# A planned two-layer transformer block: PSUM dependencies kept by bank, up and gate in banks of their own, identity products at the start, the first norm by halves

## The chip, the core and the metric

The kernel runs on one core of a Trainium2 chip. The time is device time in microseconds (us). Of the kernel before there are three runs: 910.86, 911.13 and 912.05, median 911.13. The engines are TensorE (PE; its weight loads are shown apart as PEld), VectorE (DVE), ScalarE (ACT), GpSimd (POOL), and SyncE (SP), whose queue issues the DMA transfers.

## The reference, cut to what matters

The input is x of 2 x 1024 tokens with 256 channels. Two layers follow each other; in each, attention and a feed-forward network read the same normed x and are both added to x.

```python
xn = layernorm(x)                          # layer 0
# linear attention, 16 heads of 16 channels: q' = elu(q) + 1, k' = elu(k) + 1
kv, z = sum_s k' v, q' . sum_s k'
att   = (q' kv / (z + 1e-6)) @ o_w.T + o_b
# feed-forward, 1024 wide, weights ternary: scale * round(w / scale) clipped to -1..1
ffn   = (silu(xn @ wu.T) * (xn @ wg.T)) @ wd.T      # scale = mean(|w|)
x     = x + att + ffn
xn = layernorm(x)                          # layer 1
att   = softmax(rope(q) rope(k).T / 4) v @ out_w.T + out_b
ffn   = up and gate of a signed Walsh-Hadamard transform of xn, silu(gate) * up,
        a second transform, down
x     = x + att + ffn
```

## The kernel before

Tokens are cut into four chunks of 512 (`xc[0]` to `xc[3]`, tiles x0 to x3; two for each batch). A chunk holds four groups of 128 tokens on the partitions. `norm_T` norms a chunk (DVE statistics, a power on POOL, `shift` on DVE, `xn` on ACT) and transposes it on PE into `xnT`, by way of two PSUM tiles `pt` that DVE and ACT copy out.

**The planned stage.** Everything of layer 0 but the last two feed-forward pieces, the first heads of layer 1 and the first search for peaks of scores is not issued as it is called. It is recorded: `record(group, ...)` runs a generator, and each call on PE, DVE, ACT or POOL becomes an `Op` of a `Plan` (consecutive PE calls up to a `cut` are one `Op`). `Plan.add` notes for every operation which earlier ones it needs, element by element of each tile (`Root`: writer, readers, adders). `Plan.emit` is a list scheduler: it gives each operation a length by `cost`, a hand-over by `LAT`, a priority that is its longest path to the end plus the constant that its group has for its engine in `LEADS`, and it takes a place of a tile only when its ring (`Ring`) has one free. It then issues all operations in the order found. `with_place` has an operation claim a place of a later tile already. `fetch` issues a load on SP's queue at once and notes an expected time of arrival. The list sets the order alone. The semaphores between engines come from the framework, which sees the issued order and the tiles.

In this stage the main groups are: `norm 0`, `norm 1` (the two chunks of batch 0); `project0` (`pq`, from which `r` and `e` are made on ACT and summed to q on POOL; `pkv`, from which DVE makes `kc` and ACT copies `va0`; then `ke` on ACT and `kp` on DVE); `state0` (`pk`, `kv`); `attend0` (`pa`, on DVE `rz` and `att0`; transposes to `attT`; `py`); `ternary` for `wuT0`, `wgT0` and `wdT0` (absolute values and sum on ACT, then a `pt` product over the partitions, then comparisons on DVE); the feed-forward pieces 0 to 3 with `wide=True` and 4 and 5 with `by_pool=True`; heads of layer 1 (`pqkv`, rope); the search parts.

A feed-forward piece is 256 tokens (F). `ffn0` goes over its 1024 hidden channels in blocks of 128, or in double blocks where `wide`. x is used as a sum of two single-precision-rounded parts (`xs`), so a block's up and gate are four matmuls of 256 columns each:

```python
for i in range(step):
    for w, weight in enumerate((wu, wg)):
        mm(pug[:, i, w, :], ...four products...)
scalar.activation(act, pug[:, :, 0, :], AF.Tanh, scale=su_half)
vector.scalar_tensor_tensor(act, act, 1.0, pug[:, :, 0, :], ALU.add, ALU.mult)
vector.scalar_tensor_tensor(act, pug[:, :, 1, :], sgd, act, ALU.mult, ALU.mult)
```

A wide `pug` is a `pair` tile, two PSUM banks of 512 numbers for each partition. There are two such pairs, three tiles of one bank (`bank`: `pt`, `pq`, `pkv`, `pk`, `pa`, `py`) and one, `po`.

**The main loop.** After the planned stage an order written out by hand runs eight units of attention of layer 1 (score products `scm` for the peaks, `sce` for the exponentials, `po` for the sums over v) with the rest of the feed-forward work as filler between them.

Nearly every instruction is issued through one helper, so the profile gives line L314 for all of them; groups are told apart by their tiles.

Of the kernel before, what the change touches and what calls it, by code (L numbers as in the profile page):

```python
# [21 lines left out]
P = 128  # L22
# [20 lines left out]


ENGINES = (PE, DVE, ACT, POOL)
LAT = {PE: 0.25, DVE: 0.18, ACT: 0.22, POOL: 0.15}
AHEAD = 2
LEADS = {
    "norm 0": (884, 880, 840, 780),
    "norm 1": (805, 801, 799, 770),  # L50
    "project 0": (801, 823, 823, 847),
    "project 1": (741, 1160, 919, 1000),
    "state 0": (313, 274, 323, 305),
    "attend 0": (829, 830, 806, 861),
    "attend 1": (437, 353, 368, 369),
    "wuT0": (878, 850, 751, 881),
    "wgT0": (831, 797, 770, 789),
    "wdT0": (266, 269, 300, 322),
    "piece 0": (199, 348, 389, 1041),
    "piece 1": (756, 826, 796, 770),  # L60
    "piece 2": (369, 405, 420, 380),
    "piece 3": (234, 206, 155, 167),
    "norm1 0": (367, 384, 381, 390),
    "heads 0": (303, 270, 292, 294),
    "norm1 1": (840, 853, 784, 848),
    "heads 1": (322, 272, 267, 216),
    "search 0": (216, 180, 148, 109),
    "search 1": (47, -87, 51, 13),
    "search 2": (325, 231, 328, 330),
    "search 3": (17, -6, -6, 1),  # L70
    "norm 2": (260, 224, 40, 189),
    "norm 3": (369, 226, 181, 113),
    "project 2": (245, 311, 212, 132),
    "project 3": (207, 182, 164, 210),
    "state 1": (35, 115, 42, 32),
    "attend 2": (836, 870, 861, 837),
    "attend 3": (185, 202, 198, 211),
    "piece 4": (324, 202, 297, 177),
    "piece 5": (185, 198, 238, 203),
}  # L80
FREE = ("stats", "mv", "rstd", "shift", "rz", "part")
BURST = 0.65
# [15 lines left out]
class Root:  # L98


    def __init__(self, make, n, dtype, ring, before):
        self.make, self.dtype, self.ring, self.before = make, dtype, ring, before
        self.tile = None
        self.sums = False
        self.placed = False
        self.ready = 0.0
        self.writer = np.full(n, -1)
        self.readers, self.adders, self.users = [], [], []

# [47 lines left out]
class Plan:  # L157
    def __init__(self):
        self.ops = []
        self.open = None  # L160
        self.burst = False
        self.group("norm 0")
        self.holds, self.later = [], set()

    def cut(self):
# [14 lines left out]
    def add(self, engine, call, name, args, kw):  # L180
        if engine == PE and self.open is not None:
            op = self.open
        else:
            op = Op(len(self.ops), engine, self.leads[ENGINES.index(engine)])
            self.ops.append(op)
            self.open = op if engine == PE else None
            if self.burst:
                op.cost = BURST
        op.calls.append((call, args, kw))
        for r in self.holds:  # L190
            self.use(op, r)
        self.holds.clear()
        op.needs.update(self.later)
        self.later.clear()
        outs = [args[0]] + ([kw["accum_out"]] if "accum_out" in kw else [])
        ins = [v for v in (*args[1:], *kw.values()) if isinstance(v, View) and v is not kw.get("accum_out")]
        if not self.burst:
            op.cost += cost(engine, name, outs[0], ins)
        for v in ins:
            r, ids = v.root, np.unique(v.ids)  # L200
            op.needs.update(r.writer[ids])
            if not (r.sums and outs[0].root is r):
                op.needs.update(i for i, other in r.adders if np.intersect1d(ids, other).size)
                r.readers.append((op.i, ids))
            self.use(op, r)
        for v in outs:
            r, ids = v.root, np.unique(v.ids)
            op.needs.update(r.writer[ids])
            op.needs.update(i for i, other in r.readers if np.intersect1d(ids, other).size)
            if r.sums and any(u.root is r for u in ins):  # L210
                r.adders.append((op.i, ids))
            else:
                op.needs.update(i for i, other in r.adders if np.intersect1d(ids, other).size)
                r.writer[ids] = op.i
            self.use(op, r)
        op.needs -= {-1, op.i}

    def use(self, op, r):
        op.ready = max(op.ready, r.ready)
        if r.tile is None and r not in op.roots:  # L220
            op.roots.append(r)
        r.users.append(op.i)
# [48 lines left out]
class Pool:  # L271


    def __init__(self, state, pool, bufs):
        self.state, self.pool, self.bufs, self.rings = state, pool, bufs, {}

    def tile(self, shape, dtype, tag, name, bufs=None):
        n = bufs or self.bufs
        ring = self.rings.setdefault(tag, Ring(n, tag not in ("bank", "pair", "stage", *FREE)))
        root = ring.latest = Root(  # L280
            lambda: self.pool.tile(list(shape), dtype, tag=tag, name=name, bufs=n),
            int(np.prod(shape[1:])),
            dtype,
            ring,
            ring.latest,
        )
# [52 lines left out]
def cost(engine, name, out, ins):  # L339
# [5 lines left out]
        return ins[1].ids.size * (PASS if single else COL)  # L345
    if engine == DVE:
        n = max([n] + [v.ids.size for v in ins if name in ("tensor_reduce", "bn_stats")])
        return n / 960 + 0.07 + (0.5 if name in ("tensor_scalar", "scalar_tensor_tensor") and n >= 1024 else 0.0)
    if engine == ACT:
        return n / 1200 + (0.05 if name == "copy" else 0.01 + 0.09 * len(ins))  # L350
    return n / 472 + (0.19 if n > 16 else 0.8)
# [3 lines left out]
def tile_two_layers(ctx: ExitStack, tc: tile.TileContext, a: dict, out: bass.AP):  # L355
# [10 lines left out]
    def open_pool(stack, name, bufs, **kw):  # L366
        return Pool(state, stack.enter_context(tc.tile_pool(name=name, bufs=bufs, **kw)), bufs)

    const = open_pool(ctx, "const", 1)
    small = open_pool(ctx, "small", 4)  # L370
    ps = open_pool(ctx, "ps", 1, space=PSUM)
    ident = const.tile([P, P], F32, tag="ident", name="ident")
    make_identity(nc, real(ident))
    plan = state.plan = Plan()


    def pair(name):
# [16 lines left out]
    def fetch(t, view):  # L394

        sync.dma_start(out=t, in_=view)
        fetched[0] += t.ids.size * P * 4
        t.root.ready = 3.4 + fetched[0] / 330e3

    def load_w(pool, name, k, n, tag=None):  # L400

# [10 lines left out]
        xc[c].root.sums = True  # L412
        xnT.append(const.tile([P, 2, C], F32, tag=f"xnT{c}", name=f"xnT{c}"))

    def load_x(c):
        fetch(xc[c], x_d[:, c * CT : (c + 1) * CT, :])

    ident_r = const.tile([P, P], F32R, tag="ident_r", name="ident_r")
    vector.tensor_copy(ident_r, ident)
# [1 line left out]
    vector.tensor_scalar(ones_r, ident, 0.0, 1.0, ALU.mult, ALU.add)  # L421
    minus_half = const.tile([P, CT], F32, tag="minus_half", name="minus_half")
    vector.memset(minus_half, -0.5)

    def mm(out_, pairs):
        for i, (lhsT, rhs) in enumerate(pairs):
# [3 lines left out]


    SOON, FIRST, SECOND, LAST, PAIR = 1, 2, 3, 4, 5

    def norm_T(src, dst, pause=0.0):

# [84 lines left out]
    sb = open_pool(l0, "sa", 1)  # L520


    load_x(0)
    wq = load_w(w0, "wqT0", D, D)
    qb = load(w0, "qb0", a["qb0"], [P, 2])
    minus_qb = w0.tile([P, 2], F32, tag="minus_qb", name="minus_qb")
# [34 lines left out]
    def project0(c):  # L561
# [126 lines left out]
    def ffn0(cc, before_down, wide=False, by_pool=False):  # L688
# [20 lines left out]
        for e in range(0, NB, step):  # L709
            act = (sb if wide else const).tile([P, step, F], F32, tag="act", name="act", bufs=2 if wide else 3)  # L710
            gate = const.tile([P, step, F], F32, tag="gate", name="gate", bufs=1) if by_pool else None
            if wide:
                pug = pair("pug").rearrange("p b (w n) -> p b w n", w=2)
            else:
                pug = bank("pug").rearrange("p (b w n) -> p b w n", b=1, w=2)
            for i in range(step):
                cols = slice((e + i) * P, (e + i + 1) * P)
                for w, weight in enumerate((wu, wg)):
                    if state.plan:
                        plan.with_place(act)  # L720
                        plan.with_place(gate)
                    mm(pug[:, i, w, :], [(weight[:, k, cols], xs[:, s, k, :]) for k in range(2) for s in range(2)])
                    if (i, w) != (step - 1, 1):
                        yield 4 * F * PASS
            scalar.activation(act, pug[:, :, 0, :], AF.Tanh, scale=su_half)
            if by_pool:

                scalar.mul(gate, pug[:, :, 1, :], sgd)
            if acts:
                split()  # L730
            yield 4 * F * PASS, SOON
            vector.scalar_tensor_tensor(act, act, 1.0, pug[:, :, 0, :], ALU.add, ALU.mult)
            if by_pool:
                gpsimd.tensor_tensor(act, act, gate, ALU.mult)
            else:
                vector.scalar_tensor_tensor(act, pug[:, :, 1, :], sgd, act, ALU.mult, ALU.mult)
            acts.append(act)
            yield 0.0
        before_down()
# [485 lines left out]
            plan.cut()  # L1225


    record("norm 0", norm_T(xc[0], xnT[0]))
# [168 lines left out]
```

## Time and profile before

| what | value |
|---|---|
| time, median of 3 runs | 911.13 us (910.86 to 912.05) |
| the profiled execution: its time | 910.88 us |
| the profiled execution: its span | 909.1 us (some 1.8 us lie outside it) |
| mean granted TensorE clock | 0.996 |
| PE busy in 0 to 213.0 us | 192.4 us |
| first `scm` matmul (end of the planned stage) | 213.0 us |
| HBM read, written | 11.75 MB, 2.10 MB |

A window row reads: start and end, length, then for PE, PEld, DVE, ACT and POOL the busy us and the number of instructions, then the granted clock, the DMA share and GB/s. A timeline row reads: start, duration, engine, line, operation, output <- inputs and shapes, how many; in brackets the idle time of the engine just before and what ended it. A row of the chain of waits reads: start, length, engine, tile, how many. A row of the waits reads: who waited for whom, total us, how often, the longest. Two matmul records stand for one fp32 product.

### The profile page before, as it was taken

How to read it: one execution, taken by the hardware profiler on the slowest of the kernel's cores; microseconds unless marked ns; L12 is line 12 of the kernel's file. 1: busy time of each engine (PE TensorE's matmuls, PEld its weight loads, DVE VectorE, ACT ScalarE, POOL GpSimd, SP SyncE). 2: the span in 40 equal slices, each digit the busy share in tenths (PEclk: the TensorE clock that was granted, in tenths of full speed). 3: DMA queues.
4: the chain of work that ended last, by engine and by line, in shares of the span. 5: the costliest groups of instructions: out<-in, count | busy, mean ns of one | idle time of the engine just before them, and what ended most of it. 6: DMA issues, size and time to landing. Idle time of an engine off the chain costs nothing.

```text
span 909.1 us, 14565 instructions
## 1 busy us (share of the span) xinstructions
PE 863.3 (95%) x6036; PEld 515.5 (57%) x6036; DVE 581.9 (64%) x954; ACT 439.2 (48%) x641; POOL 212.1 (23%) x279
## 2 busy tenths in 40 slices
PE   5988899999989998999999999999999999999997
PEld 2687766676556543554555555555555555555543
DVE  3895558886876786657765656677565666656212
ACT  5733565434655542444544444455444444444563
POOL 2525578433643140005500000154000000000000
PEclk9999999999999999999999999999999999999999
DMA  9100000000000110000000000000000000000001
GB/s 316 64 1 1 1 1 1 1 1 1 1 25 25 47 47 1 1 1 1 1 1 1 1 1 25 1 1 1 24 1 1 1 2 1 1 1 2 1 6 41
DMA packets 11297, 14.77 MB, mean 16 GB/s; under 512 B 1248, under 2 KB 8928, under 8 KB 11232
## 3 DMA queue, kind: packets, MB, share of 16 engines
q1 hardware_dynamic: 11232, 13.85, 4.6%
q8 instruction: 47, 0.77, 0.4%
q14 instruction: 18, 0.15, 0.1%
HBM read 11.75 MB, written 2.10 MB: 15 GB/s over the span
## 4 chain that ended last, share of the span: by engine, by line
PE 72%; DVE 21%; issue 3%; ACT 3%; DMA 1%; POOL 0%; SPq 0%; ACTq 0%; DVEq 0%; POOLq 0%
PE pug L314 19%; DVE peak L314 17%; PE scm L314 16%; PE py L314 13%; PE sce L314 7%; PE pqkv L314 4%; PE pt L314 4%; PE pkv L314 3%; PE pw L314 2%; PE po L314 2%; PE pq L314 1%; PE sc L314 1%; ACT pr L314 1%; DVE act L314 1%; ACT act L314 1%
## 5 line engine op out<-in xcount | busy, mean ns | idle before, releaser
L314 ACT ACTIVATE pr<-sce 128x1024 f32<-128x1024 f32 x256 | 260.2, 1023 | 269.4 <-PE sce L314 269.1
L314 DVE TENSOR_REDUCE peak<-scm 128x2 f32<-128x1024 f32 x224 | 274.0, 1223 | 167.6 <-PE scm L314 166.7
L314 PE MATMUL po<-pr,va 128*17 128x512 f32 x1024 | 135.6, 598 | 0.0
L314 PE MATMUL sce<-qk_hi 32*128 32x512 f32 x512 | 123.0, 495 | 4.7 <-ACT pr L314 2.3
L314 PEld LDWEIGHTS scm<-qk_hi 32*128 32x128 f32 x448 | 41.4, 182 | 151.4 <-DVE peak L314 113.8
L314 PE MATMUL scm<-qk_hi 32*128 32x512 f32 x448 | 111.9, 496 | 12.0 <-DVE peak L314 1.0
L314 POOL CAST tops<-nm 128x16 fp32r<-128x16 f32 x16 | 3.4, 213 | 409.4 <-DVE nm L314 405.6
L314 PE MATMUL sce<-ql,qk_hi 32*128 32x512 f32 x512 | 97.0, 393 | 0.0
L314 PE MATMUL sce<-mx,ones_r 32*128 32x512 f32 x512 | 96.7, 391 | 0.1
L314 PE MATMUL scm<-qk_hi,ql 32*128 32x512 f32 x448 | 89.1, 394 | 0.0
L314 DVE SCALAR_TENSOR_TENSOR act<-act,pug 128x256 f32<-128x256 f32 (+1 forms) x112 | 50.8, 454 | 58.2 <-ACT act L314 32.6
L314 PE MATMUL pug<-xnT,eff_wgT 128*128 128x256 f32 x256 | 69.2, 392 | 0.0
L314 PE MATMUL pug<-xnT,eff_wuT 128*128 128x256 f32 x256 | 68.3, 382 | 0.0
L314 PE MATMUL py<-wd,hid 128*128 128x256 f32 x256 | 63.2, 388 | 0.0
L314 POOL TENSOR_TENSOR hid<-act,hid 128x256 fp32r<-128x256 f32 (+1 forms) x48 | 44.1, 921 | 68.9 <-ACT hid L314 40.7
L314 ACT ACTIVATE act<-pug,ws_ug 128x256 f32<-128x256 f32 x64 | 30.3, 474 | 55.3 <-PE pug L314 55.3
L314 PEld LDWEIGHTS pug<-xnT,eff_wgT 128*128 128x128 f32 x256 | 45.5, 189 | 16.5 <-issue 10.6
L314 PEld LDWEIGHTS py<-wd,hid 128*128 128x128 f32 x256 | 46.4, 190 | 14.8 <-issue 8.6
L314 PEld LDWEIGHTS sce<-qk_hi 32*128 32x128 f32 x512 | 45.9, 181 | 15.6 <-ACT pr L314 9.7
L314 PEld LDWEIGHTS pug<-xnT,eff_wuT 128*128 128x128 f32 x256 | 47.9, 190 | 9.8 <-issue 2.6
L314 PEld LDWEIGHTS sce<-mx,ones_r 32*128 32x128 f32 x512 | 46.6, 183 | 11.0 <-ACT mx L314 0.5
L314 PE MATMUL pqkv<-wqkvT,xnT 128*128 128x384 f32 x128 | 49.0, 505 | 2.2 <-DVE ql L314 1.6
(144 smaller groups left out, 1310.4 us busy)
## 6 DMA issues: line engine op xcount, KB each, us to landing
x<-in_x SPq DMA_DIRECT2D x4, 512.0 KB, 7.1
out<-x SPq DMA_DIRECT2D x16, 128.0 KB, 1.7
both<-in_wuT SPq DMA_DIRECT2D x1, 1024.0 KB, 8.6
both<-in_wgT SPq DMA_DIRECT2D x1, 1024.0 KB, 10.7
wdT<-in_wdT SPq DMA_DIRECT2D x1, 1024.0 KB, 13.0
raw<-in_wdT SPq DMA_DIRECT2D x2, 512.0 KB, 3.5
raw<-in_wgT SPq DMA_DIRECT2D x2, 512.0 KB, 3.4
raw<-in_wuT SPq DMA_DIRECT2D x2, 512.0 KB, 3.3
```

Of the source, the lines that this page charges most:

```text
L314: return call(*map(real, args), **{k: real(v) for k, v in kw.items()})
```

## The change

- `open_pool` and `Pool` hand a `grain` to each `Root`. For the PSUM pool it is 512 (C), a bank; the plan's dependencies of PSUM tiles are then noted by bank and no longer by element. Arrival times (`ready`) are noted for each element.
- In `ffn0` a wide block's `pug` is laid out with up first (all of bank 0) and gate second (all of bank 1), and the loops are exchanged: up of both halves, then gate of both.
- Fourteen fp32 products of `ident` with itself go to PE ahead of the plan, which is now created after them.
- `xc[0]` is loaded in two transfers and normed by `norm_halves`: two token groups at a time, from the statistics to the transposed copy (DVE copies the first half, ACT the second).
- `cost` has other lengths for long DVE operations, `LAT` has 0.1 in place of 0.15 for POOL, `project0` calls `with_place` for q, `kc` and `va0`, and all constants of `LEADS` are new.

```diff
-LAT = {PE: 0.25, DVE: 0.18, ACT: 0.22, POOL: 0.15}
+LAT = {PE: 0.25, DVE: 0.18, ACT: 0.22, POOL: 0.1}
 LEADS = {
-    "norm 0": (884, 880, 840, 780),
-    "norm 1": (805, 801, 799, 770),
-    "project 0": (801, 823, 823, 847),
+    "norm 0a": (1268, 1283, 1353, 1307),
+    "norm 0b": (1266, 1278, 1247, 1252),
+    "norm 1": (1210, 1162, 1187, 1148),
+    "project 0": (1056, 1212, 1220, 1354),
...
         for v in ins:
-            r, ids = v.root, np.unique(v.ids)
+            r, ids = v.root, np.unique(v.ids // v.root.grain)
...
-        return n / 960 + 0.07 + (0.5 if name in ("tensor_scalar", "scalar_tensor_tensor") and n >= 1024 else 0.0)
+        if n >= 1024 and name != "tensor_reduce":
+            return 0.85 if name == "tensor_scalar" else 1.8
+        return n / 960 + 0.07
...
-    ps = open_pool(ctx, "ps", 1, space=PSUM)
+    ps = open_pool(ctx, "ps", 1, C, space=PSUM)
...
-    plan = state.plan = Plan()
...
+    warm = bank("warm")
+    for _ in range(14):
+        tensor.matmul(warm[:, 0:P], lhsT=ident, rhs=ident, start=True, stop=True)
+    plan = state.plan = Plan()
...
+    def norm_halves(src, dst):
...
+        xn = at.tile([P, CT, D], F32, tag="stage", name="xn", bufs=3)
+        for a in range(0, CT, 2):
+            two = slice(a, a + 2)
+            for j in range(a, a + 2):
+                vector.bn_stats(stats[:, j, :], src[:, j, :])
+                vector.bn_aggr(mv[:, j, :], stats[:, j, :])
+            vector.tensor_scalar_add(rstd[:, two], mv[:, two, 1], LN_EPS)
+            gpsimd.tensor_tensor(rstd[:, two], rstd[:, two], minus_half[:, two], ALU.pow)
+            vector.scalar_tensor_tensor(shift[:, two], mv[:, two, 0], -1.0, rstd[:, two], ALU.mult, ALU.mult)
+            for j in range(a, a + 2):
+                scalar.activation(
+                    xn[:, j, :], src[:, j, :], AF.Identity, bias=shift[:, j : j + 1], scale=rstd[:, j : j + 1]
+                )
+            pt = bank("pt").rearrange("p (k n) -> p k n", k=2)
+            for j in range(2):
+                for k in range(2):
+                    tensor.transpose(pt[:, k, j * P : (j + 1) * P], xn[:, a + j, k * P : (k + 1) * P], ident)
+            (scalar.copy if a else vector.tensor_copy)(dst[:, :, a * P : (a + 2) * P], pt)
+            yield
...
-    load_x(0)
+    load_x(0, parts=2)
...
         for m in range(2):
+            plan.with_place(q0[c])
             pq = bank("pq")
...
         for j in range(CT):
+            plan.with_place(kc)
+            plan.with_place(va0[b])
             pkv = bank("pkv")
...
             if wide:
-                pug = pair("pug").rearrange("p b (w n) -> p b w n", w=2)
+                pug = pair("pug").rearrange("p w (b n) -> p w b n", b=2)
...
-            for i in range(step):
-                cols = slice((e + i) * P, (e + i + 1) * P)
-                for w, weight in enumerate((wu, wg)):
+            for w, weight in enumerate((wu, wg)):
+                for i in range(step):
+                    cols = slice((e + i) * P, (e + i + 1) * P)
...
-            scalar.activation(act, pug[:, :, 0, :], AF.Tanh, scale=su_half)
+            scalar.activation(act, pug[:, 0, :, :], AF.Tanh, scale=su_half)
```

More of the change, by code (lines that the diff above doesn't have):

```diff
@@ L45 @@
 ENGINES = (PE, DVE, ACT, POOL)
-LAT = {PE: 0.25, DVE: 0.18, ACT: 0.22, POOL: 0.15}
+LAT = {PE: 0.25, DVE: 0.18, ACT: 0.22, POOL: 0.1}
 AHEAD = 2
 LEADS = {
-    "norm 0": (884, 880, 840, 780),
-    "norm 1": (805, 801, 799, 770),
-    "project 0": (801, 823, 823, 847),
[L52 to L79, printed above, removed]
@@ new lines @@
+    "norm 0a": (1268, 1283, 1353, 1307),
+    "norm 0b": (1266, 1278, 1247, 1252),
+    "norm 1": (1210, 1162, 1187, 1148),
+    "project 0": (1056, 1212, 1220, 1354),
+    "project 1": (981, 1355, 1139, 1289),
+    "state 0": (594, 645, 635, 642),
+    "attend 0": (974, 935, 955, 963),
+    "attend 1": (417, 552, 629, 461),
+    "wuT0": (1187, 1197, 1154, 1169),
+    "wgT0": (1364, 1352, 972, 1039),
+    "wdT0": (535, 515, 586, 606),
+    "piece 0": (460, 529, 461, 589),
+    "piece 1": (1299, 1282, 1268, 1287),
@@ new lines @@
+    "piece 2": (1099, 767, 1229, 1058),
+    "piece 3": (965, 967, 900, 942),
+    "norm1 0": (889, 872, 881, 927),
+    "heads 0": (969, 1023, 971, 1088),
+    "norm1 1": (921, 944, 969, 1152),
+    "heads 1": (951, 921, 937, 944),
+    "search 0": (588, 645, 635, 630),
+    "search 1": (692, 602, 631, 644),
+    "search 2": (639, 616, 689, 676),
+    "search 3": (1243, 1270, 1288, 1295),
+    "norm 2": (568, 534, 523, 547),
+    "norm 3": (948, 938, 972, 960),
+    "project 2": (654, 696, 637, 632),
@@ L80 @@
+    "project 3": (572, 548, 504, 552),
+    "state 1": (571, 611, 558, 597),
+    "attend 2": (1173, 1369, 1172, 1236),
+    "attend 3": (644, 574, 633, 573),
+    "piece 4": (906, 1076, 609, 921),
+    "piece 5": (1168, 1568, 1476, 1520),
 }
@@ L98, with __init__ @@
 class Root:
-    def __init__(self, make, n, dtype, ring, before):
-        self.make, self.dtype, self.ring, self.before = make, dtype, ring, before
+    def __init__(self, make, n, dtype, ring, before, grain):
+        self.make, self.dtype, self.ring, self.before, self.grain = make, dtype, ring, before, grain
         self.tile = None
@@ L105, in __init__ @@
         self.placed = False
-        self.ready = 0.0
+        self.ready = np.zeros(n)
         self.writer = np.full(n, -1)
@@ L161, in __init__ @@
         self.burst = False
-        self.group("norm 0")
+        self.group("norm 0a")
         self.holds, self.later = [], set()
@@ L199, in add @@
         for v in ins:
-            r, ids = v.root, np.unique(v.ids)
+            r, ids = v.root, np.unique(v.ids // v.root.grain)
             op.needs.update(r.writer[ids])
+            op.ready = max(op.ready, r.ready[ids].max())
             if not (r.sums and outs[0].root is r):
@@ L206, in add @@
         for v in outs:
-            r, ids = v.root, np.unique(v.ids)
+            r, ids = v.root, np.unique(v.ids // v.root.grain)
             op.needs.update(r.writer[ids])
@@ L218, in use @@
     def use(self, op, r):
-        op.ready = max(op.ready, r.ready)
         if r.tile is None and r not in op.roots:
@@ L271, with __init__ @@
 class Pool:
-    def __init__(self, state, pool, bufs):
-        self.state, self.pool, self.bufs, self.rings = state, pool, bufs, {}
+    def __init__(self, state, pool, bufs, grain):
+        self.state, self.pool, self.bufs, self.rings, self.grain = state, pool, bufs, {}, grain
     def tile(self, shape, dtype, tag, name, bufs=None):
@@ L285, in tile @@
             ring.latest,
+            self.grain,
         )
@@ L364, in tile_two_layers, with open_pool @@
     )
-    def open_pool(stack, name, bufs, **kw):
-        return Pool(state, stack.enter_context(tc.tile_pool(name=name, bufs=bufs, **kw)), bufs)
+    def open_pool(stack, name, bufs, grain=1, **kw):
+        return Pool(state, stack.enter_context(tc.tile_pool(name=name, bufs=bufs, **kw)), bufs, grain)
     const = open_pool(ctx, "const", 1)
     small = open_pool(ctx, "small", 4)
-    ps = open_pool(ctx, "ps", 1, space=PSUM)
+    ps = open_pool(ctx, "ps", 1, C, space=PSUM)
     ident = const.tile([P, P], F32, tag="ident", name="ident")
     make_identity(nc, real(ident))
-    plan = state.plan = Plan()
     def pair(name):
@@ L397, in fetch @@
         fetched[0] += t.ids.size * P * 4
-        t.root.ready = 3.4 + fetched[0] / 330e3
+        t.root.ready[t.ids] = 3.4 + fetched[0] / 330e3
     def load_w(pool, name, k, n, tag=None):
@@ L413, in tile_two_layers, with load_x @@
         xnT.append(const.tile([P, 2, C], F32, tag=f"xnT{c}", name=f"xnT{c}"))
-    def load_x(c):
-        fetch(xc[c], x_d[:, c * CT : (c + 1) * CT, :])
+    def load_x(c, parts=1):
+        n = CT // parts
+        for j in range(0, CT, n):
+            fetch(xc[c][:, j : j + n, :], x_d[:, c * CT + j : c * CT + j + n, :])
     ident_r = const.tile([P, P], F32R, tag="ident_r", name="ident_r")
@@ L432, in tile_two_layers @@
     SOON, FIRST, SECOND, LAST, PAIR = 1, 2, 3, 4, 5
+    def norm_halves(src, dst):
+        stats = small.tile([P, CT, 6], F32, tag="stats", name="stats")
+        mv = small.tile([P, CT, 2], F32, tag="mv", name="mv")
+        rstd = small.tile([P, CT], F32, tag="rstd", name="rstd")
+        shift = small.tile([P, CT], F32, tag="shift", name="shift")
+        xn = at.tile([P, CT, D], F32, tag="stage", name="xn", bufs=3)
[17 more added lines that the diff above has]
+            yield
     def norm_T(src, dst, pause=0.0):
@@ L712, in ffn0 @@
             if wide:
-                pug = pair("pug").rearrange("p b (w n) -> p b w n", w=2)
+                pug = pair("pug").rearrange("p w (b n) -> p w b n", b=2)
             else:
-                pug = bank("pug").rearrange("p (b w n) -> p b w n", b=1, w=2)
-            for i in range(step):
-                cols = slice((e + i) * P, (e + i + 1) * P)
-                for w, weight in enumerate((wu, wg)):
+                pug = bank("pug").rearrange("p (w b n) -> p w b n", b=1, w=2)
+            for w, weight in enumerate((wu, wg)):
+                for i in range(step):
+                    cols = slice((e + i) * P, (e + i + 1) * P)
                     if state.plan:
@@ L721, in ffn0 @@
                         plan.with_place(gate)
-                    mm(pug[:, i, w, :], [(weight[:, k, cols], xs[:, s, k, :]) for k in range(2) for s in range(2)])
+                    mm(pug[:, w, i, :], [(weight[:, k, cols], xs[:, s, k, :]) for k in range(2) for s in range(2)])
                     if (i, w) != (step - 1, 1):
                         yield 4 * F * PASS
-            scalar.activation(act, pug[:, :, 0, :], AF.Tanh, scale=su_half)
+            scalar.activation(act, pug[:, 0, :, :], AF.Tanh, scale=su_half)
             if by_pool:
-                scalar.mul(gate, pug[:, :, 1, :], sgd)
+                scalar.mul(gate, pug[:, 1, :, :], sgd)
             if acts:
@@ L731, in ffn0 @@
             yield 4 * F * PASS, SOON
-            vector.scalar_tensor_tensor(act, act, 1.0, pug[:, :, 0, :], ALU.add, ALU.mult)
+            vector.scalar_tensor_tensor(act, act, 1.0, pug[:, 0, :, :], ALU.add, ALU.mult)
             if by_pool:
@@ L735, in ffn0 @@
             else:
-                vector.scalar_tensor_tensor(act, pug[:, :, 1, :], sgd, act, ALU.mult, ALU.mult)
+                vector.scalar_tensor_tensor(act, pug[:, 1, :, :], sgd, act, ALU.mult, ALU.mult)
             acts.append(act)
@@ L1225, in record @@
             plan.cut()
-    record("norm 0", norm_T(xc[0], xnT[0]))
+    halves = norm_halves(xc[0], xnT[0])
+    for group in ("norm 0a", "norm 0b"):
+        plan.group(group)
+        next(halves)
+        plan.cut()
     record("norm 1", norm_T(xc[1], xnT[1]))
```

## The prediction

> **What bounds the kernel now.** I read the page first (engines, then slices), then the windows by stage, the timeline of the start and of one feed-forward stretch, and the waits. The page says who carries the span:
>
> ```profile
> PE 863.3 (95%) x6036; PEld 515.5 (57%) x6036; DVE 581.9 (64%) x954; ACT 439.2 (48%) x641; POOL 212.1 (23%) x279
> PE   5988899999989998999999999999999999999997
> ```
>
> TensorE (PE) is the bound nearly everywhere; in the 40 slices of 22.7 us only the first and the third to fifth fall to 8 or below. The two programs have the same order of instructions on every engine from the first score matmul (`scm`) on, at 213.0 us. Only the stage before it can change; the other 696.1 us of the span are taken over. The windows of that stage (columns: length, then busy us of PE, weight load, DVE, ACT, POOL):
>
> ```profile
> 0.00:10.00 10.00, 1.27 (x3) 0.55 (x3) 5.25 (x25) 3.24 (x5) 2.79 (x10) 1.00 0.77 237
> 10.00:25.00 15.00, 13.90 (x38) 7.38 (x38) 4.88 (x11) 11.06 (x24) 6.26 (x6) 1.00 1.06 380
> 25.00:50.00 25.00, 24.80 (x137) 17.77 (x136) 22.02 (x53) 16.13 (x31) 11.31 (x8) 1.00 0.08 23
> 50.00:75.00 25.00, 21.97 (x152) 19.90 (x151) 21.45 (x54) 7.70 (x13) 9.34 (x8) 1.00 0.00 1
> 75.00:100.00 25.00, 19.97 (x159) 18.78 (x158) 12.38 (x24) 12.51 (x22) 12.91 (x12) 1.00 0.01 1
> ```
>
> PE is idle at the start, full at 25 to 50 (where DVE, 22 of 25, is nearly full too), and loses 8 us at 50 to 100. I give every PE instruction of this stage its shortest repeated spacing in the trace (a 256-column matmul record 0.108 us, a 512-column one 0.429 us); they sum to 183.3 us. The rest, 213.0 - 183.3 = 29.7 us, is lag, and where it grows is what can be won: 14.2 us by 20 us, flat to 50, 15.7 at 55, 27.2 at 110, flat to 180, 29.7 at 205.
>
> The start, in the timeline and the chain of waits:
>
> ```profile
> 4.59 1.41 DVE L314 BATCH_NORM_STATS2 stats<-x 128x6 f32<-128x256 f32 x4 [1.65 <-DMA x<-in_x]
> 6.57 1.03 POOL L314 TENSOR_TENSOR rstd<-rstd,minus_half 128x4 f32<-128x4 f32 x1 [5.00 <-DVE minus_qb L314]
> 8.05 2.07 ACT L314 ACTIVATE xn<-x,shift,rstd 128x256 f32<-128x256 f32 x4 [2.12 <-DVE shift L314]
> 10.69 0.69 DVE L314 COPY xnT<-pt 128x512 f32<-128x512 f32 x1 [0.24 <-PE pt L314]
> ```
> ```profile
> 12.59 3.78 PE pkv L314 x4
> 17.88 5.15 PE pkv L314 x12
> ```
>
> A serial chain over four engines, then four `pkv` records at 0.945 us where twelve later ones take 0.429 us each: PE ran at half clock up to about 17.5 us.
>
> The growth from 55 to 110 is a wait that repeats:
>
> ```profile
> 66.47 0.63 PE L314 MATMUL pug<-xs,t_wgT 128*128 128x256 f32 x4
> 67.20 0.69 ACT L314 ACTIVATE act<-pug,su_half 128x512 f32<-128x512 f32 x1 [1.44 <-POOL hid L314]
> 67.94 0.74 PE L314 MATMUL pug<-xs,t_wgT 128*128 128x256 f32 x4 [0.84 <-ACT act L314]
> ```
> ```profile
> PEld pug L314 <- ACT act L314: 9.0, 9, 1.0
> ```
>
> Of a wide double block the second gate group stands still while ACT takes the tanh of up: 1.00 us of PE in each of eight blocks. With three weaker ones (0.40, 0.56, 0.40) that is 9.36 us over sixteen blocks.
>
> **The change part by part.**
>
> *First norm by halves, x0 in two transfers.* The packets of x0's first 256 KB end near 3.33 us and all 512 KB at 4.02, some 0.5 before the landing, so the first half is there at about 3.85 (0.7 earlier). Its stats (2 x 0.35), aggregates (2 x 0.09) and rstd (0.17) end near 5.1, the power of POOL (1.03) at 6.2. Now its `shift` waits in DVE's queue behind the stats of the second half, `minus_qb`, and the copies `ident_r` and `ones_r` (0.22 and 0.23): about 6.75. ACT's four `xn` (0.52 each) run 6.95 to 9.03 instead of 8.05 to 10.12. The copy of the first transposed half stands behind three stats of x1 (0.37 each; x1 lands later by the 0.45 us of one more issue on SP): to 9.4. First `pkv` at about 9.45, before 12.59: 3.1 us earlier. SP's extra issue moves all later loads by 0.45; the ternary weights are needed later than they land, hidden.
>
> *Fourteen identity products.* They need only `ident`. By the half-clock spacing (0.853 per 512-column record, two records a product) a 128-column product takes 0.43, so 14 end at 7.4 at the latest (5.7 if the clock rises after about 3.4); the first transpose is ready at 7.5. They delay nothing. They would raise the clock before `pkv` and save 4 x (0.945 - 0.43) = 2.1 us; but between their end and 9.45 PE has just eight transposes. The trace of before shows the clock at half for 3.41 us from 253.07 and from 348.64, each after a window with 1.6 to 2.0 us idle. So it may fall again; I count half of the gain, the end points are 0 and 2.1.
> The Trainium skill, "TensorE: Matmul & The Clock Gate", Part 1, says the same against these products: the gate watches free-running windows of about 3.4 us, and a transpose does not count as busy; by it alone the whole gain is lost.
>
> *What becomes of that lead.* The four `pkv` tiles of x0 end near 17.9, before 22.9: 5 us ahead. Then it is no longer PE that is late. The new list puts the absolute values of `wuT0` and `wgT0` (1.05 each), the relus and exps of q and the `va0` copies into one ACT queue, and `kc` (0.42), ternary comparisons (0.75, and 1.28 to 2.33) and `kp` into DVE's. The PSUM ring of three banks couples them: `pkv` waits for ACT's copies. Walking the new queues with these durations, the matmul on the second partial sum waits for ACT's last `wgT0` half, and the lead is 2.65 at 44 us. Then comes a stretch where the new list gives DVE more than before: for PE work 20 to 40 us it has 25.5 us of DVE work (x3's and x2's stats, `kv`, and the `rz`/`att0` triples), before 20.3. I walk waits of 0.65, 0.9, 1.6, 0.4 and 1.15 us there. At PE work 39.2 the lag is 15.4 to 17.6, where before had 15.7 at the same work: -0.3 to +1.9, and I take **+1.0**, above the middle, because a walk leaves out hand-overs.
>
> *Up and gate in banks of their own; the list counts by bank.* In the list's books tanh now frees nothing that gate needs. But the built program still has the wait: in eight blocks of the new order tanh is issued between the two gate groups, waits for the first and holds the second, as the tile is one tile for its guard. So eight times 1.00 us remain (tanh 0.69 plus hand-over). In six more the list lets some matmuls between; subtracting those (0.108 to 0.118 each) leaves 0.15, 0.5, 0.5, 0.5, 0.8 and 0.5. Two blocks have none. 8.0 + 2.95 = 10.95 against 9.36: **+1.5** (+0.5 if four of the six are hidden, +2.0 if none).
> The page "PSUM — Partial Sum Buffer", section "PSUM bank collisions raise a hardware error", says that different banks may be used by two engines at once, so the chip itself would allow what the guard forbids; by it alone the sum would fall by up to 9.4 us.
>
> *Other waits at 50 to 130.* Before has 0.93, 0.75, 0.76 and 0.40 us outside these blocks, 2.8 in all. In the new order I find short-covered places only of 0.24 and 0.35. Some I will have missed: **-0.6** (0 to -2.2).
>
> *The end of the stage.* Before loses 2.7 us at 180 to 205, in waits of 0.48, 0.49, 0.38, 0.67 and smaller. After ends on eight `py` of attention, whose fourth waits for a bank behind a peak reduction and x additions of DVE (0.75), and on the peak transposes (0.2 to 0.4): 1.0 seen, an unseen rest. **0** (-1.7 to +1.2). `with_place` and the new costs act only through the order.
>
> **Sum:** 1.0 + 1.5 - 0.6 + 0 = +1.9 us on the profiled execution's 910.88, 912.8. That execution lies 0.25 under the median 911.13, so the forecast is **913.0**. About 0.2% (1.8 us) is what a measurement of this kernel tells from no change: 909.3 to 912.95 is "same". The forecast sits on its upper edge, its own range is 910.5 to 915.
>
> **The rivals.**
> *The lead lasts (faster).* If DVE and ACT keep up, the 2.65 to 5 us arrive at the wide blocks. For it: PE was 24.8 of 25 busy there before, so PE work begun earlier should end earlier. Against: DVE is at 22 of 25 and gets more. Price: -2.65 or -5 in place of +1.0, so -1.75 to -4.1, about 908. It decides from the point where DVE's extra 5 us in that stretch fall into gaps. Chance 0.22.
> *The chip or guard lets the gate groups go (much faster).* The change would do what its list believes; 1.0 - 9.4 - 0.6 gives 902. Against: the wait is in the built program. Chance 0.05.
> *DVE becomes the bound at 35 to 60 (slower).* Its 5.2 us of extra work come out in full, with the partly covered gates uncovered: 5.2 + 2.0 - 0.6, about 917.5. For it: 22.0 and 21.5 of 25 busy. Chance 0.20.
> *A clock window falls or is spared in the main loop.* 1.7 us each way, as the phase of the stage's end moves: 911.3 or 914.7. Chance 0.08.
> The forecast case has 0.45.
>
> **How the numbers follow.** Faster: 0.22 of the lasting lead less 0.02, 0.05 of the gates, a share of 0.05 from the rest: 0.30. Slower: 0.20, 0.24 of the forecast case, 0.04 of the clock: 0.48. Same: 0.22. The range 906 to 918 leaves out the freed gates, the largest lead and the worst DVE stretch.
>
> **What would show it.** Right: first `pkv` near 9.5; lag in the wide blocks still growing by 1.00 us at eight gate groups with the tanh as releaser; the first `scm` at 214 to 216. Wrong: no ACT wait at gate groups; or first `pkv` after 11; or lag at 55 us (PE work 39) under 13, which would be the lasting lead; or over 19, the DVE case.

## The result and the profile after

After runs in 913.84 us, before in 910.98 (medians of 18 runs each, taken together): the ratio is 1.0034, 95% interval 1.0021 to 1.0047. The forecast was 913.0. The profiled execution of after took 912.87 us with a span of 911.1, that of before 910.88 with 909.1: +1.99 us.

The page of after, engines and slices, answers to the same lines of before: PE has 4.7 us more (the products alone are 5.17), and the first slice goes from 5 to 8.

```profile
PE 868.0 (95%) x6064; PEld 518.4 (57%) x6064; DVE 584.2 (64%) x956; ACT 440.6 (48%) x641; POOL 214.7 (24%) x280
PE   8988999999989998999999999999999999999997
```

The windows of after (the same columns as before): PE gains 5.7 us in the first ten, then 25 to 50 falls from 24.80 to 22.03 and 50 to 75 from 21.97 to 20.31, with DVE at 22.78 of 25 in the first of these.

```profile
0.00:10.00 10.00, 6.92 (x36) 5.78 (x36) 5.28 (x22) 3.36 (x5) 2.42 (x10) 1.00 0.68 211
10.00:25.00 15.00, 14.01 (x41) 6.90 (x42) 8.64 (x21) 13.59 (x27) 3.49 (x3) 1.00 1.06 380
25.00:50.00 25.00, 22.03 (x124) 15.79 (x122) 22.78 (x69) 12.72 (x25) 15.10 (x11) 1.00 0.11 33
50.00:75.00 25.00, 20.31 (x147) 18.50 (x146) 17.30 (x35) 8.64 (x15) 10.78 (x7) 1.00 0.00 1
75.00:100.00 25.00, 22.12 (x171) 20.84 (x170) 12.20 (x24) 14.93 (x27) 15.09 (x13) 1.00 0.00 1
```

The start of after in the timeline (start, duration, engine):

```profile
1.47 5.17 PE L316 MATMUL warm<-ident 128*128 128x128 f32 x28 [1.47 <-POOL ident masks.py:199]
8.59 1.08 DVE L316 BATCH_NORM_STATS2 stats<-x 128x6 f32<-128x256 f32 x3 [1.64 <-DMA x<-in_x]
9.59 0.67 DVE L316 COPY xnT<-pt 128x512 f32<-128x512 f32 x1
10.31 5.42 PE L316 MATMUL pkv<-wkvT,xnT 128*128 128x512 f32 x12 [0.95 <-DVE xnT L316]
```

Twelve `pkv` records in 5.42 us are 0.45 each: PE runs at full clock from the first. They begin at 10.31, not at 9.45, because the copy into `xnT` stands behind statistics of x1, and these can start only at 8.59, when x1 has landed, instead of at 7.20.

Up to PE work 6 us that is a lead of 4.70 us over before; by work 34 it is gone. The four longest idle times of PE between 34 and 50 us end on DVE three times and on ACT once:

```profile
34.81 1.19 PE L316 MATMUL pk<-va,kp 128*128 128x136 f32 x8 [0.38 <-DVE kc L316]
37.29 3.05 PE L316 MATMUL pk<-va,kp 128*128 128x136 f32 x24 [0.34 <-ACT r L316]
42.72 0.93 PE L316 MATMUL pa<-kv,q 128*128 128x136 f32 x6 [0.52 <-DVE kv L316]
47.94 0.70 PE L316 MATMUL pa<-kv,q 128*128 128x136 f32 x4 [1.01 <-DVE rz L316]
```

A wide block of after, and the row of the waits over the planned stage, read as in before: tanh between the two gate groups, and the second held for it.

```profile
56.23 0.63 PE L316 MATMUL pug<-xs,t_wgT 128*128 128x256 f32 x4
56.95 0.69 ACT L316 ACTIVATE act<-pug,su_half 128x512 f32<-128x512 f32 x1 [1.45 <-PE pug L316]
57.69 0.74 PE L316 MATMUL pug<-xs,t_wgT 128*128 128x256 f32 x4 [0.84 <-ACT act L316]
```
```profile
PEld pug L316 <- ACT act L316: 9.5, 10, 1.0
```

The first `scm` comes at 216.04 us, before at 213.02: +3.02. The main loop has the same instructions and took 695.0 instead of 696.1: the clock record of after has one window of 3.41 us at half clock in it (at 350.0), that of before two (253.1 and 348.6). So +3.02 - 1.05 = +1.97, the difference of the profiled executions. Runs at one mean granted clock compare without those windows: at 0.996 before is 911.57 (39 runs) and after 913.84 (5 runs), +2.3.

### The profile page after: what moved, and what is told of

Read it like the earlier page. It is cut to its first block, busy times and chain, and to the rows that moved or that the text cites. A ratio compares the mean times of both kernels' runs of the same rounds, so it can differ in the third digit from the quotient of the medians.

```text
span 911.1 us, 14625 instructions
## 1 busy us (share of the span) xinstructions
PE 868.0 (95%) x6064; PEld 518.4 (57%) x6064; DVE 584.2 (64%) x956; ACT 440.6 (48%) x641; POOL 214.7 (24%) x280
## 4 chain that ended last, share of the span: by engine, by line
PE 69%; DVE 21%; ACT 4%; issue 2%; POOL 2%; DMA 1%; SPq 0%; ACTq 0%; POOLq 0%; DVEq 0%
PE pug L316 19%; DVE peak L316 16%; PE scm L316 16%; PE py L316 12%; PE sce L316 7%; PE pqkv L316 4%; PE pt L316 4%; PE pw L316 2%; PE sc L316 2%; PE po L316 2%; ACT pr L316 1%; ACT act L316 1%; DVE act L316 1%; DMA x<-in_x 1%; PE pq L316 1%
## 5 line engine op out<-in xcount | busy, mean ns | idle before, releaser
L316 PEld LDWEIGHTS sce<-qk_hi 32*128 32x128 f32 x512 | 45.8, 181 | 15.8 <-ACT pr L316 9.9
L316 ACT ACTIVATE act<-pug,su_half 128x256 f32<-128x256 f32 (+1 forms) x48 | 26.1, 546 | 52.1 <-PE pug L316 44.8
## 6 DMA issues: line engine op xcount, KB each, us to landing
both<-in_wgT SPq DMA_DIRECT2D x1, 1024.0 KB, 10.4
```

The source lines that it names most:

```text
L316: return call(*map(real, args), **{k: real(v) for k, v in kw.items()})
```

## The experiments

All kernels are read in the prediction's terms: lag (time less PE work at full speed) at four points of PE work, which every order passes, and the time of the first `scm`. The lag at work 6 holds the start, the clock, and the landing of x1, which differs between executions: 7.13 to 8.73 us in the five kernels that load x0 in one transfer, 7.18 to 9.30 in the nine that load it in two. The experiments are therefore compared by how much the lag grows from work 6 on. Lags and `scm` times are of one profiled execution each; medians are of all runs, and each ratio is against the runs of before beside them (medians 910.79 to 911.02).

| kernel | lag at 6 | at 39.2 | at 80 | at the end | first `scm` | median us | ratio to before, 95% |
|---|---|---|---|---|---|---|---|
| before | 14.24 | 15.61 | 27.17 | 29.62 | 213.02 | 910.98 | |
| after | 9.54 | 15.89 | 26.78 | 32.64 | 216.04 | 913.84 | 1.0034 (1.0021 to 1.0047) |
| gate_first | 9.01 | 15.38 | 18.77 | 24.90 | 208.31 | 904.08 | 0.9936 (0.9917 to 0.9955) |
| before_gate_first | 13.73 | 15.44 | 18.77 | 23.58 | 206.98 | 905.48 | 0.9946 (0.9926 to 0.9967) |
| no_products | 11.71 | 17.68 | 28.61 | 34.43 | 217.84 | 915.23 | 1.0057 (1.0038 to 1.0076) |
| before_start | 11.91 | 16.18 | 28.04 | 30.66 | 214.06 | 911.74 | 1.0024 (1.0009 to 1.0040) |
| before_layout | 16.16 | 17.53 | 29.09 | 31.49 | 214.90 | 910.90 | 1.0003 (0.9989 to 1.0017) |
| short_stats | 11.19 | 16.21 | 27.11 | 33.50 | 216.90 | 913.94 | 1.0027 (1.0013 to 1.0042) |
| short_adds | 10.28 | 14.80 | 25.71 | 31.52 | 214.93 | 912.16 | 1.0012 (0.9997 to 1.0027) |
| after_old_leads | 13.33 | 18.14 | 26.09 | 32.68 | 216.08 | 912.36 | 1.0012 (0.9994 to 1.0030) |
| by_element | 9.31 | 16.82 | 26.71 | 42.50 | 225.91 | 924.26 | 1.0145 (1.0127 to 1.0163) |
| gate_first_adds | 9.42 | 14.53 | 17.96 | 23.62 | 207.03 | 904.53 | 0.9936 (0.9919 to 0.9953) |
| before_gate_first_adds | 15.83 | 18.10 | 21.44 | 26.30 | 209.70 | 905.90 | 0.9954 (0.9940 to 0.9969) |
| before_gate_first_products | 15.03 | 16.72 | 20.09 | 25.00 | 208.40 | 905.37 | 0.9952 (0.9935 to 0.9968) |

**Is the guard by tile, and what does it cost?** In `before_layout` only the places of up and gate in the pair are changed (and the loops that fill it).

> The kernel before with only the layout of a wide pug changed: all up in the first bank, all gate in the second. No queue changes its order. Theory (the guard ties the whole tile): the same eight waits of 1.00 us, stage end 213.0 within 0.3, no change of time. Rival (the guard works by banks): no gate group waits for the tanh, stage end near 205.

```diff
-                pug = pair("pug").rearrange("p b (w n) -> p b w n", w=2)
+                pug = pair("pug").rearrange("p w (b n) -> p w b n", b=2)
...
```

From work 6 to the end it gains 15.33 us of lag, before 15.38. The waits of its stage read as in before:

```profile
PEld pug L314 <- ACT act L314: 8.9, 9, 1.0
```

So up and gate in banks of their own bring nothing: the guard ties the tile. (Its first `scm` is 1.9 later because of the start of this execution: x1, from a load that neither kernel changes, landed at 8.73 us instead of 7.17, which put the first `pkv` at 14.14 instead of 12.59, and the clock rose at 19.85 instead of 17.55.)

`gate_first` leaves the tile and changes the order of issue: the rest of gate goes ahead of the tanh.

> The kernel after, with one thing moved: in each of its sixteen wide blocks the remaining gate products are issued ahead of the tanh of up instead of behind it, so that nothing in the built program holds gate back; the queues of DVE, POOL and ACT keep their order. Theory (the tile is guarded as one, and the wait costs what it shows): no gate group waits for ACT, about 10.4 us of waits go, tanh starts up to 0.5 us later per block; the planned stage ends near 207 instead of 216.0 us and the time falls by 8 to 10 us, to about 905 (ratio to before 0.993). Rival (the elementwise chain of ACT, DVE and POOL is nearly as long as PE there, so half comes back as waits for hid or for a free pair): end near 211, time about 909.

```diff
...
+        for act in [op for op in order if op.tanh]:
+            at = order.index(act)
+            late = [op for op in order[at:] if op.engine == PE and act.tanh in op.writes]
+            for op in late:
+                order.remove(op)
+            order[at:at] = late
         for op in order:
```

Its timeline at the same block: eight gate records without a gap, tanh behind them, and PE already in the next block.

```profile
55.72 1.09 PE L327 MATMUL pug<-xs,t_wgT 128*128 128x256 f32 x8
56.66 1.09 PE L327 MATMUL pug<-xs,t_wuT 128*128 128x256 f32 x8
56.91 0.69 ACT L327 ACTIVATE act<-pug,su_half 128x512 f32<-128x512 f32 x1 [1.92 <-PE pug L327]
```

Lag from work 39.2 to 80 grows by 3.4 instead of 10.9. Of the 10.4 us of waits 7.2 net stay gone after work 6; others stand in the place of the rest, `py` that waits for `hid` from POOL and one `pqkv`:

```profile
PE py L327 <- POOL hid L327: 1.1, 3, 0.4
PE pqkv L327 <- ACT xnT L327: 1.0, 1, 1.0
```

With 904.08 us it has the lowest median here (`gate_first_adds`, 904.53, is not told from it), 6.7 us under the runs of before beside it (910.79) and 9.8 under after. The theory's time (905) holds; its waits did not all turn into time. The end of the stage moved by 7.73 us (9 expected). The rest of the 9.8 goes at least in part with the clock: six of the eighteen runs of after had a mean granted clock of 0.994, none of `gate_first` was under 0.996. At 0.998 `gate_first` took 904.21 us (3 runs) and after 912.74 (6 runs), 8.5 apart.

> The same move in the kernel before (gate of both halves ahead of the tanh, all constants and the layout of before). Theory: its eight waits of 1.00 us and 0.56 and 0.40 go; planned stage ends near 205 instead of 213.0 us, time near 902.5 (ratio 0.991). Rival (the chain gives half back): 209, time about 907.

The same edit in before: 905.48 us and a first `scm` at 206.98, between theory (902.5, 205) and rival (907, 209). From work 6 on, 5.5 of its 9.4 us are gone; the rest comes back as waits for `hid` and others.

**What the start brings.** The products are left out of after:

> The kernel after without the fourteen identity products; all else the same. The trace of after has the clock full from 5.2 us on. Theory (the lead is used up by DVE and ACT before 50 us, so what the products save is hidden): half clock up to the end of the first busy window, the first pkv records at 0.85 us, lag at PE work 8 us higher by 2 us, but at PE work 39 by no more than 0.5; time within 0.5 us of after. Rival (PE is what is late at the start): the 2.1 us stay to the end, time 2 us above after.

```diff
-    warm = bank("warm")
-    for _ in range(14):
-        tensor.matmul(warm[:, 0:P], lhsT=ident, rhs=ident, start=True, stop=True)
```

The rival is right: 2.17 us at work 6, still 1.79 at 39.2 and 1.79 at the end; the median is 1.4 us above that of after. What is late at the start is passed on nearly whole. Not all of the 2.17 is the products' doing: x1 landed 0.53 us later in this execution (9.09 instead of 8.56), and the first `pkv` came 0.53 later (10.84). The clock, at half until 14.19, makes the other 1.6. That a late start is passed on speaks against a DVE that sets a fixed time: its work hangs on the products of PE, and both shift together.

> The kernel before with only the new start: x0 in two transfers, first norm by halves, fourteen identity products; its own constants, dependencies and layout. Theory (DVE and ACT set the pace from 25 to 55 us in any order): first pkv near 10.3 us, the lead of 4.7 us shrinks to 0 or 1 by PE work 39, planned stage ends at 212 to 213, time 0 to 1 us below before. Rival (the lead lasts where the old order of the list gives DVE less at that place): the stage ends at 208.5 to 210 and the time falls by 3 to 4.5 us, and then it is the new constants that lose it.

The edit is that of the change's diff: two loads, `norm_halves`, the products. With before's own constants the lead is given back too: 11.91 against 14.24 at work 6, but 16.18 against 15.61 at 39.2. The first `scm`, at 214.06, is 1.04 later than before, beyond the theory's 213, and the time 0.24% longer (0.09 to 0.40). So the lead is lost without the new constants. It is not shown that every order loses it: the list made another one here than in before (on DVE the second subtraction of `wgT` stands behind those of `wuT`, at 39.95 us instead of 29.44). A half-clock window of 3.41 us began at 11.0 us; the products had not held the clock, which costs an estimated 1.7 us (half of it) by work 6.

**Is it DVE that takes the lead?** Both kernels keep every queue of after and shorten some operations; what they compute is told in the expectations. The diffs show what each edit comes to.

> The kernel after; the eight first-norm statistics of x2 and x3 (38 to 44 us on DVE, 0.35 us each) read 16 of the 256 channels, so chunks 2 and 3 are normed by the wrong statistics; the order of every queue is that of after. It takes 8 x 0.3 = 2.4 us out of DVE in the stretch where DVE has no gap (28 to 55 us). Theory (DVE is what is late there): lag at PE work 39 falls from 15.9 to 13.5 to 14, and the planned stage ends 1.5 to 2.4 us earlier than 216.0. Rival (the waits of PE there come from ACT or from the ring of banks): no change at PE work 39, end within 0.4 us.

```diff
-            vector.bn_stats(stats[:, j, :], src[:, j, :])
+            vector.bn_stats(stats[:, j, :], src[:, j, 0:16])   # x2, x3
```

> The kernel after; the four additions of the bias ob to x0 and x1 on POOL cover 16 of the 256 channels (the bias is left out of the rest); the order of every queue is that of after. In after the two wgT comparisons took 1.48 and 1.42 us and the two ternary subtractions 2.11 and 1.95 us while POOL was busy all the time from 30 to 35 us, where the same operations took 0.75 and 1.29 us for wuT beside an idle POOL. Theory (DVE runs slower beside POOL, and DVE is what is late): those four fall by up to 2.9 us together, lag at PE work 39 by 2 to 2.9, the stage ends near 213.5. Rival (something else made them longer, or DVE has slack later): durations or end unchanged.

```diff
-            gpsimd.tensor_tensor(x2, x2, ob.unsqueeze(1).to_broadcast([P, 2, D]), ALU.add)
+            gpsimd.tensor_tensor(x2[:, :, 0:16], ...)          # x0, x1
```

Of the four `wgT` operations on DVE the first comparison and the first subtraction, in after and then in `short_adds` (timeline: start, duration):

```profile
29.07 1.48 DVE L316 TENSOR_SCALAR t_wgT<-both,sc_wgT 128x1024 fp32r<-128x1024 f32 x1
32.32 2.11 DVE L316 SCALAR_TENSOR_TENSOR t_wgT<-both,sc_wgT,t_wgT 128x1024 fp32r<-128x1024 f32 x1
```
```profile
29.84 0.75 DVE L325 TENSOR_SCALAR t_wgT<-both,sc_wgT 128x1024 fp32r<-128x1024 f32 x1
31.68 1.29 DVE L325 SCALAR_TENSOR_TENSOR t_wgT<-both,sc_wgT,t_wgT 128x1024 fp32r<-128x1024 f32 x1
```

All four together fell by 2.89 us (6.96 to 4.07), with POOL out of the way. From work 6 to 39.2 lag grows by 6.35 in after, 5.02 in `short_stats`, 4.52 in `short_adds`: 1.3 of 2.4 us and 1.8 of 2.9 come through. Both began later than after (11.19 and 10.28 at work 6; in `short_stats` a half-clock window at 10.6, in `short_adds` x1 landed at 9.30), so a part of that could be less lead to lose: `no_products`, 2.17 later, lost 0.38 less. Taking that share off leaves about 1.0 and 1.7. To the end of the stage 0.8 and 1.9 us are left of the gain (lag growth of 22.3 and 21.2 us against 23.1); because of the later starts the first `scm` came at 216.90 and 214.93, where the theories had 213.6 to 214.5 and 213.5, and the medians are 913.94 and 912.16. DVE is late there, and POOL beside it makes it later, but neither explains the whole 5 us.

**Who makes the loss after 110 us?** From work 80 to the end lag grows by 2.5 in before, 2.6 in `before_start`, 5.9 in after.

> The kernel after with the constants of LEADS of before (both halves of the norm with those of norm 0); start, layout, bookkeeping by bank, the costs and the claims of places are those of after. Theory (the scattered waits after 110 us belong to the new constants' order): lag from PE work 85 to 160 flat within 1 us as in before, where after gains 4.6; the stage ends at 212 to 214.5. Rival (the bookkeeping or the costs make them): it ends at 215.5 or later, with the lag growing in the same stretch.

Its diff is the table of LEADS alone, put back. From work 80 on the lag grows by 6.6, of it about 3 us from 85 to 160: the theory falls. The end of the stage, 216.08, would not show it alone, since two half-clock windows from 9.5 us on put the lag at work 6 at 13.33, 3.8 above after. The old constants under the new costs, books and claims lose as much in this last part; between 39.2 and 80 they lose 8.0 us instead of 10.9. The profiled execution is 2.1 us shorter than that of after with the same first `scm`: its main loop, which has no half-clock window, took 692.9 us instead of 695.0. At a granted clock of 0.998 three runs took 909.2 to 909.8 us, six of after 911.7 to 913.2.

> The kernel after with the list's PSUM dependencies by element again (grain 1); all else, the layout of up and gate too, as in after. Theory (the guard ties the tile whatever the list books, and in the new layout up and gate are apart in both accounts): the same eight waits of 1.00 us, stage end 215 to 217, time within 1 us of after. Rival (the books by bank shape the order of the rest): waits elsewhere change by 2 us or more in sum.

```diff
-    ps = open_pool(ctx, "ps", 1, C, space=PSUM)
+    ps = open_pool(ctx, "ps", 1, space=PSUM)
```

Here the rival is right: 15.8 us from work 80 on, and all four runs lie between 922.6 and 925.5. In the profiled execution some 4 of the 15.8 us are the clock: it was at half from 194.78 to 205.02 us, and PE was busy for 8.17 us of that. The rest are waits, one of 2.07 us of idle PE before a `pa` at 199.14 among them. Between 39.2 and 80 it gains 9.9, much as after; the loss is behind that, which suggests that the new constants fit the books that they came with. Which of costs, books by bank and `with_place` makes the 3.4 us of after could not be told apart: it stays open. The waits of PE in after from 107 to 213 us are small ones, by different releasers; the longest:

```profile
PE pug L316 <- DVE act L316: 0.6, 1, 0.6
PE pug L316 <- DVE kc L316: 0.5, 2, 0.3
PE pkv L316 <- ACT va L316: 0.4, 1, 0.4
```

**Can it be bettered?** `plan.behind` holds the four additions in the list until the weights are ternary, on top of the gate edit; for this the `ternary` groups are recorded ahead of `attend`.

> The kernel of gate_first with the four bias additions to x0 and x1 on POOL held until wgT is ternary (each waits for the group that writes it); the other queues keep their order. Theory (POOL beside DVE costs DVE 2.9 us at 29 to 37 us, and DVE is late there): the four wgT operations take 0.75 and 1.29 us, lag at PE work 39 falls by 1.5 to 2 against gate_first (15.4), stage end 206.3 to 207.3, time near 902.5. Rival (the additions now slow the attention group's DVE work behind them as much): end within 0.4 us of 208.3.

```diff
+            if c < 2:
+                plan.behind(tern["wgT0"])
             gpsimd.tensor_tensor(x2, x2, ob.unsqueeze(1).to_broadcast([P, 2, D]), ALU.add)
...
```

Two additions still ran beside DVE at 28.6 us, since the list holds the order only and POOL's queue came to them early; the subtractions fell to 1.28, the comparisons stayed at 1.47 and 1.43. Lag at work 39.2 is 0.85 lower (1.5 to 2 expected), the first `scm` 1.28 earlier, as expected; the median, 904.53 against 904.08 with 6 runs each, does not show it.

> The same hold of the four additions in the kernel of before_gate_first (until wuT, the later of the two there, is ternary). There two of three slowed operations (2.12 and 1.96 us) stand beside the additions. Theory: lag at PE work 39 falls by 1 to 2 from 15.4, stage end 205 to 206 (from 207.0), time near 904. Rival: unchanged within 0.4 us.

Rival: from work 6 on 10.5 us of lag against 9.9, no gain (905.90). One subtraction still took 2.23, now beside the sums of q.

> The kernel of before_gate_first with the fourteen identity products and without the norm by halves. The products end near 6.7 us, the first pkv comes at 12.6: 2 us of idle PE, then eight transposes in 2.8 us, then 1 us idle. Theory (a gap of that length lets the clock fall, as 3.41 us at half clock near 10 us showed in before_start and after_old_leads): the pkv records are at half clock in most executions, lag at PE work 6 is 13 to 13.7, stage end within 0.7 us of 207.0. Rival (the clock holds): lag at PE work 6 near 11.7, end near 205.

The theory holds in kind, not in size: the clock was full at 5.07 us and fell for two windows from 11.9 on. Lag at work 6 is 15.03 (13 to 13.7 expected), the first `scm` at 208.40 (at most 207.7 expected), the time unchanged (905.37 against 905.48).

## Why the prediction held, and where it did not

The sum was +1.9 us on the profiled execution, measured +1.99; the median +2.86. Of its own signs, the first `pkv` (10.31) lies between right (near 9.5) and wrong (after 11), the gate groups wait as it said, and the first `scm` (216.04) is at the upper end of 214 to 216. Its terms, from the lags of the two profiled executions:

| term | forecast | measured |
|---|---|---|
| start, to PE work 39.2 | +1.0 | +0.28 |
| gate waits behind it (8.96 before, 10.42 after) | +1.5 | +1.46 |
| other waits to work 80 | -0.6 | -1.74 |
| the rest of the stage, gates left out | 0 | +3.02 |
| main loop | 0 | -1.05 |

- **The gate waits** were right in cause and size: eight of 1.00 (tanh between the groups) and 0.53, 0.57, 0.53 and 0.79 where some matmuls cover. `before_layout` shows the cause, `gate_first` the price. The page "PSUM — Partial Sum Buffer" of the Trainium skill, section "PSUM bank collisions raise a hardware error", lets two engines use different banks at once; no run here shows that, because the guard of the built program does not allow it.
- **The start** was right in kind: 4.70 us of lead at PE work 6 (forecast 5), 1.0 left at 44 us (forecast 2.65), gone by work 34. In its parts the landing of x1 was mis-sized (1.4 us later, forecast 0.45), which put the first `pkv` at 10.31; that landing differs by as much between executions of kernels with the same loads, so the +0.28 is in part chance. The products kept the clock full for all `pkv` in this execution, where half of that was counted: 2.1 us by the text's price, some 1.6 by `no_products`. That DVE paces the stretch is supported by two runs, for about 1.0 and 1.7 us; that it does so whatever PE brings is refuted by `no_products`, where 1.79 of 2.17 us reach the end.
- **The end of the stage** is the step that failed. The text listed 1.0 us of waits in the new order, set them against the 2.7 of before, and took 0 with a top of +1.2; it was +3.0. A reading of the order does not show small waits: after has eleven of 0.24 to 0.59 us between 110 and 215 us, behind ever other engines. Before has small ones there too, but after's come early: 0.29, 0.25, 0.59, 0.38 and 0.39 us from 113 to 131 us, where before has one of 0.40 apart from its gate waits. What puts them there, costs, books by bank or claims of places, stays open. No rival named them.
- **The main loop** was priced at 1.7 us each way in a rival, and this time it gave 1.05 back. It has one half-clock window fewer there. The stage alone moved by +3.02, the medians by +2.86. That the profiled sum met its figure is so in part luck: +3.02 at the end, against -1.14 in the other waits, -0.72 in the start and -1.05 in the loop.
- **The rivals**: the lead did not last; no gate group was let go; the bound by DVE did not come out in full.
- **Readings that were off**: slices 12 and 16 of before stand at 8 too; the main loop's two half-clock windows lie in them. The 256-column records of `pug` stand 0.113 us apart at the closest and mostly 0.116 to 0.120, not 0.108; the lags here go with the larger spacing. By the text's own 0.43 us a product and a clock that rises 3.4 us behind their start, the products end at 6.2, not 5.7; they ended at 6.64. That a transpose does not count as busy stands in Part 4 of the page on TensorE, and its Part 1 lets the clock fall after an idle window, so "the whole gain is lost" does not follow from that page alone.

## What to carry to other kernels

A list scheduler's book of dependencies has to match what the guard in the built program enforces; a finer book makes it issue a reader between two writers of the same tile, and each such place that nothing covered cost 1.00 us of PE here. Look in the built order for waits that the list believes away, and move the writers ahead of the reader: that one edit, without any change of layout or constants, took 7.2 us of lag out of after and 5.5 out of before, for waits of 10.4 and 9.4 us (1.0% and 0.5% of the time). A lead won at the start is worth what the next stage can take; measure the lag at equal work, not at equal time.

## What the runs showed of the hardware

- A second engine on the same stretch of time: POOL's 128x512 additions beside DVE lengthen DVE's 128x1024 comparison from 0.75 to 1.48 us and its subtraction from 1.28 to 2.11.
- Whether a burst of products holds the clock differs from execution to execution. Of nine profiled kernels with the fourteen products, five kept the full clock up to `pkv` (after among them), and four fell to half for one or two windows of 3.41 us from 9.5 to 11.9 us on. After, `short_adds` and `short_stats` issue the same start, and only the last of them fell. The products began at 1.46 or 1.47 us in all nine, and the clock rose between 5.07 and 7.56; without them it rose anywhere from 14.2 to 19.9. The Trainium skill, "TensorE: Matmul & The Clock Gate", Part 1, has a free-running window of about 3.4 us, and these runs agree. It lets the clock fall after an idle window; here the windows before the four falls were not idle (PE busy for 1.75 to 2.09 of 3.41 us, transposes among it). Whether a transpose counts as busy they do not decide.
- Each such window costs what it halves: before at a mean granted clock of 1.000 took 907.94 us (10 runs), at 0.998 910.29 (17), at 0.996 911.57 (39). That is 3.6 us of spread from the clock alone, more than this change moves.
- x0 in two transfers of 256 KB puts the issue of x1, queued behind it, 0.46 us later (2.73 instead of 2.27). In the two profiled executions x1 landed 1.4 us later, but that is not the price of the split: x1 landed at 7.13 to 8.73 us in the five kernels without it (median 7.32) and at 7.18 to 9.30 in the nine with it (median 8.51). Why it differs so, no run tells.
